# Seven products of quarter blocks in place of the last block products of a Strassen-Winograd convolution

## The chip, the cores and the metric

The kernel runs on one core of one Trainium2 chip, in 32-bit floating point. The metric is device time in microseconds for one launch, from the kernel's start to its end on that core; lower is better. Times of a kernel are the median of several runs; the profile is of one further execution.

## The reference

The input `x` has 8 images of 512 channels and 32 x 32 pixels. What is computed, cut to the steps that matter:

```
def _L0_conv_ref(x, ...):
    t = cbs(x, cv1_w, cv1_bn, 0)              # 1x1 convolution 512 -> 512, scale and shift, silu
    ys = [t[:, :C], t[:, C:]]                 # C = 256
    for i in range(2):
        yi = ys[-1]
        z = cbs(yi, m_cv1_w[i], m_cv1_bn[i], 1)           # 3x3 convolution 256 -> 256
        z = bot_attention(z, m_qkv_w[i], m_rw[i], m_rh[i]) # 4 heads of 64 over 1024 pixels
        z = silu(bn_eval(conv2d(z, m_cv2_w[i], 0), m_cv2_bn[i]))
        ys.append(yi + z)
    return cbs(concatenate(ys, axis=1), cv2_w, cv2_bn, 0)  # cv2: 1x1 convolution 1024 -> 512
x = x + _L0_conv_ref(_gn(x), ...)             # _gn: group norm
```

The change lies in the last convolution, `cv2`. Per image it is a matrix product: a weight matrix of 512 x 1024 times the four parts `ys` (1024 channels x 1024 pixels).

## The kernel before

The images are worked on in four pairs (`p` = 0 to 3, images `ia` and `ib`), one pair after another in straight code. Within a pair the order on TensorE is: 3x3 convolution 1 of both images (`conv3x3`, in a transformed domain, with loaded weights `u`), projection and attention 1 of `ia`, the same for `ib`, convolution 2, attention 2 of `ia` and of `ib`, and `cv2` of both. Where a fourth pair follows, the first 1x1 convolution `cv1` of the next pair is worked in between.

`cv2` of one image is done by Winograd's form of Strassen's method: the 512 x 1024 weights are cut into 2 x 2 blocks of 256 x 512, and the activations into 2 x 2 blocks of 512 channels x 512 pixels (`top` and `bottom`). Seven block products replace eight. Their weights are three raw blocks (`11`, `12`, `22`) and four sums (`s1` to `s4`); on the other side stand three raw blocks and the sums `t1` to `t4`. One block product (`product`, line 1338) is 8 matmuls of 128 x 128 weights by 512 columns, into one PSUM tile of two banks (`ps[:, o, :]`, one bank for each half of the outputs). Each matmul shows as two records in the profile. PSUM has three such tiles under the tag `big` and one under `av`.

For pairs 0 to 2 the function `strassen` makes the seven products in the order `11`, `s1`, `12` with `s4`, `s2`, `s3`, `22` (parts `part1`, `part2`, `part3`); it is called for `ia` first (`a1` to `a3`) and then for `ib` (`b1` to `b3`). After each of the last three, VectorE adds the whole PSUM tile to a running sum `m1` (lines 1414, 1418 and 1421, 1024 elements a partition), and lines 1416 and 1419 form two of the four output blocks from it. `finish` then applies the scale, shift and silu on ScalarE, and GpSimd's queue adds `x` with an accumulating DMA (line 1388) and stores the result (line 1389).

In the last pair (called the tail here), `rest_apart` does the same in separate steps: `m2_m3`, `m6` (`s2`), `m7` (`s3`), `m4` (`22`) for `ia`, and for `ib` `m6`, `m7` and then `m4_pieces`, which makes `22` in one piece of 512 columns and two of 256 (line 1514). The adds are lines 1493, 1498 and 1503, and 1519 for the pieces. In the tail the residual `x` of `ib` is loaded whole beforehand (`whole`, four tiles) and added on VectorE (line 1556).

Behind `b3` of pairs 0 to 2 follows the input transform of the next pair's convolution (`tiles_steps`, lines 565 to 614), on VectorE, with two small memsets on GpSimd (lines 575 and 576) for each tile of rows `w_rows`. Its third part (`i` = 2) is traced after `b3`, and its output needs the memory (`v`) that holds `y3b`, an operand of `ib`'s products `12` and `s4`.

The order on each engine is not that of the source alone. A planner goes through the program with its own estimates of durations and issues on each engine, out of what is ready by then, what comes first in the source; `tc.issue_after` adds an order by hand. The order that comes out is fixed: on the chip each engine goes through its queue in that order, and an instruction that waits holds up all behind it. The planner also puts in the waits, and gives tiles of the same tag their memory in turn. The tag `u` (`ring`) has 10 places of 4 KB a partition; weights of all kinds go through it.

Of the kernel before, what the change touches and what calls it, by code (L numbers as in the profile page):

```python
# [52 lines left out]
P = 128  # L53
# [8 lines left out]
def kernel(  # L62
# [51 lines left out]
    def ring(shape, name):  # L114
        return const.tile(shape, F32, tag="u", name=name, bufs=RING)
# [170 lines left out]
    def make_ws(a):  # L286
# [11 lines left out]

        return {f"s{i + 1}": w for i, w in enumerate(sums)}, part1, part2

    fed = {}

    def loader(key):
        kind = key[0]
        if kind == "u":
            _, n, oc, i, cp = key
            w = ring([P, NM, 2, 2, P], "u")
            nc.sync.dma_start(w, u_dram[n][oc][i][cp])
        elif kind == "sq":
            _, n, _, j = key  # L310
            at, size = SQ[j]
            w = ring([P, size, 3, P], "sq")
            nc.sync.dma_start(w, sq_dram[n][:, at : at + size])
        elif kind == "sw":
            at, size = SQ[key[2]]
            w = ring([P, size, NX // 2, C], "sw")
            nc.sync.dma_start(w, sw_dram[:, at : at + size])
        elif kind == "w1":
            w = ring([P, NX // 2, 2 * C], "w1")
            nc.sync.dma_start(w, cv1_w.rearrange("(k p) o -> p k o", p=P)[:, ts(key[2], NX // 2)])  # L320
        elif kind == "qkv":
            w = ring([P, 3 * C], "w_qkv")
            nc.sync.dma_start(w, m_qkv_w[key[1], ts(key[3], P), :])
        elif kind == "w2":
# [172 lines left out]
    def stages(act, small, ps_big, ps_av, n_pt):  # L497
# [843 lines left out]
                            skip_group_check=onto,  # L1341
                        )

        def strassen(b, ws, top, tags, tile_of):

            kept = {}

# [43 lines left out]
            def part3(bottom, after=None):  # L1391
                t1 = kept["t1"]
                t2, t3 = sums_tile("k"), tile_of("t3").rearrange("p a c (h w) -> p a c h w", w=F)
                with tc.issue_after(after.ins) if after else nullcontext():
                    for part in range(2):
                        tt(t2[:, part], bottom[1][part], t1[:, part], ALU.subtract)
                    for part in range(2):
                        tt(t3[:, part], bottom[1][part], top[1][part], ALU.subtract)
                t4 = sums_tile("q")
                for part in range(2):  # L1400
                    tt(t4[:, part], t2[:, part], bottom[0][part], ALU.subtract)
# [60 lines left out]

            return SimpleNamespace(m1=m1, t1=t1, m5=m5, kept=kept)

        def rest_apart(ws, kept, bottom, t2, t3, t4, new, finish):

            m1, m5 = kept["m1"], kept["m5"]
            pss, c12 = {}, []

            def raw(name, src, outs=range(2)):  # L1470
                if name not in pss:
                    pss[name] = ps_big.tile([P, 2, HALF], F32, tag="big", name="c_new")
                product(pss[name], ws(name), src, outs=outs)
                return pss[name]

            def m2_half():
                raw("12", bottom[0], [0])

            def m2_m3():
                raw("12", bottom[0], [1])  # L1480
                raw("s4", bottom[1])

            def add_m2():
                c11 = new()
                tt(c11, pss["12"], m1, ALU.add)
                finish(0, c11)

            def add_m3():
                c12.append(new())
                tt(c12[0], pss["s4"], m5, ALU.add)  # L1490

            def m6():
                tt(m1, raw("s2", t2), m1, ALU.add)
                tt(c12[0], c12[0], m1, ALU.add)
                finish(1, c12[0])

            def m7():
                tt(m1, raw("s3", t3), m1, ALU.add)
                tt(m5, m5, m1, ALU.add)
                finish(2, m5)  # L1500

            def m4():
                tt(m1, m1, raw("22", t4), ALU.subtract)
                finish(3, m1)

            def m4_pieces(out_of):
                flat = lambda ap: ap.rearrange("p c h w -> p c (h w)") if len(ap.shape) == 4 else ap
                t4s = [flat(t) for t in t4]
                places = [(0, 0, HALF), (1, 0, HALF // 2), (1, HALF // 2, HALF // 2)]
                for o, at, size in places:  # L1510
                    pool, tag = (ps_av, "av") if (o, at) == (1, 0) else (ps_big, "big")
                    ps = pool.tile([P, HALF], F32, tag=tag, name="c_new")[:, :size]
                    for k in range(KB):
                        nc.tensor.matmul(
                            ps, ws("22")[:, k, ts(o, P)], t4s[k // NM][:, k % NM, at : at + size],
                            start=(k == 0), stop=(k == KB - 1),
                        )
                    src = m1[:, o, at : at + size]
                    tt(src, src, ps, ALU.subtract)
                    out_of(3, o, at, size, src)  # L1520

            return SimpleNamespace(
                m2_half=m2_half, m2_m3=m2_m3, add_m2=add_m2, add_m3=add_m3, m6=m6, m7=m7, m4=m4, m4_pieces=m4_pieces
            )

        C_BLOCKS = ((0, 0), (0, 1), (1, 1), (1, 0))
# [497 lines left out]
    for p in range(NP):  # L2024
# [392 lines left out]
        if not more:  # L2417
# [14 lines left out]
            whole = [ring([P, HW], "x_res") for _ in range(NO)]  # L2432
            for oc in range(NO):
                nc.sync.dma_start(whole[oc], x[ib, ts(oc, P), :])
            ts_a = [], [], []
            rest_a = s.rest_apart(w_of, heads[ia].kept, bottom_a, *ts_a, acc_tile, s.finish_apart(ia))
# [29 lines left out]
            rest_b = s.rest_apart(w_of, heads[ib].kept, bottom, *ts_b, lambda: kept_sums.pop(0), finish)  # L2466
# [7 lines left out]
            rest_b.m2_m3()  # L2474
            rest_b.add_m2()
            rest_b.add_m3()
            rest_b.m6()
# [23 lines left out]
        b1, b1_more, b2, b3 = s.strassen(ib, w_of, top, {"m1": ("p3", 1), "m5": ("p4", 1)}, tile_of)  # L2501
        b1()
        b1_more()
        b2()
        vs = v_units()
        ecs = [{}, {}]
        for g in range(G):
# [119 lines left out]
```

## Time and profile before

| what | value |
| --- | --- |
| median of 3 runs | 2220.57 us (2220.26 to 2220.92) |
| profiled execution | 2222.78 us; its span 2221.2 us, the rest lies around it |
| TensorE (PE) busy | 2192.8 us, 99% of the span |
| VectorE (DVE) busy | 1752.2 us, 79% |
| ScalarE (ACT) busy | 1093.9 us, 49% |
| GpSimd (POOL) busy | 222.0 us, 10% |
| granted TensorE clock | 0.998 |

A busy share is that of the whole span; stages differ. PEld is TensorE's weight load, which runs beside matmuls. In a timeline a row is: start, length, engine, line, operation, output<-inputs, sizes, count, and in square brackets the idle time before it with what ended it. In a table by stage it is: from:to, length, busy time of each engine with its count of instructions, clock, the DMA engines' busy share, and GB/s.

### The profile page before, as it was taken

To read this page: it belongs to the slowest core of one execution; us is meant where nothing else is said; L and a number is where in the kernel's file an instruction comes from. 1 tells how busy PE (TensorE), PEld (TensorE's weight loads), DVE (VectorE), ACT (ScalarE), POOL (GpSimd) and SP (SyncE) were. 2 spreads that over 40 slices of the span, in tenths; PEclk is the share of its full clock that TensorE was granted. 3 is DMA by queue.
4 is the path that set the end of the run, shared out by engine and by line. 5 is a ranking of instruction groups with operands and counts; after the bars stand their busy time and mean duration, and the time that the engine had idled before them with its cause. 6 is when DMAs were issued, how large, how long until landed. Compare 5 with 4: busy or idle time off the path is not lost.

```text
span 2221.2 us, 40357 instructions
## 1 busy us (share of the span) xinstructions
PE 2192.8 (99%) x16330; PEld 1079.8 (49%) x16330; DVE 1752.2 (79%) x2794; ACT 1093.9 (49%) x1320; POOL 222.0 (10%) x416
## 2 busy tenths in 40 slices
PE   7999999999999999999999999999999999999998
PEld 3653437343474444734447443654344734383433
DVE  8988879878769688977857868987785877897664
ACT  7454553554225666465323676455622465336543
POOL 4322210000220000000021000000002100000001
PEclk9999999999999999999999999999999999999999
DMA  8954447312582324512268141542126701261123
GB/s 265 317 170 136 168 149 260 105 64 68 142 264 68 119 82 132 199 59 68 63 162 267 31 166 36 190 131 77 58 67 171 268 30 44 91 208 34 58 59 96
DMA packets 133799, 285.61 MB, mean 129 GB/s; under 512 B 33541, under 2 KB 61185, under 8 KB 132581
## 3 DMA queue, kind: packets, MB, share of 16 engines
q1 hardware_dynamic: 101700, 197.34, 26.9%
q0 software_dynamic: 31904, 85.61, 13.2%
q8 instruction: 131, 2.15, 0.4%
q14 instruction: 64, 0.52, 0.1%
HBM read 214.86 MB, written 68.03 MB: 127 GB/s over the span
## 4 chain that ended last, share of the span: by engine, by line
PE 90%; DVE 6%; issue 1%; DMA 1%; ACT 1%; POOL 0%; DVEq 0%; ACTq 0%; POOLq 0%
PE av_ps L1101 19%; PE l_ps L1064 18%; PE c_ps L659 10%; PE c L1338 9%; PE c_new L1338 8%; PE p_ps L940 7%; PE m_ps L1318 5%; PE x_ps L1579 4%; PE ps L529 4%; PE p_ps L946 3%; PE s_ps L1119 1%; DMA taps<-in_m_cv_w_dram 1%; DVE acc L1085 1%; PE p_ps L904 1%; PE pv_ps L946 0%
## 5 line engine op out<-in xcount | busy, mean ns | idle before, releaser
L1068 ACT ACTIVATE pt<-l_ps 128x1024 f32<-128x1024 f32 x512 | 495.7, 1023 | 328.1 <-PE l_ps L1064 252.2
L1064 PE MATMUL l_ps<-q,kr 64*64 64x512 f32 x4096 | 485.5, 590 | 0.9 <-ACT pt L1068 0.9
L1101 PE MATMUL av_ps<-pt,vT 64*64 64x512 f32 x4096 | 484.7, 590 | 1.3 <-DVE z L1109 1.1
L1085 DVE TENSOR_TENSOR acc<-acc,pt 128x1024 f32<-128x1024 f32 x362 | 442.8, 1223 | 37.6 <-ACT pt L1068 11.2
L1101 PEld LDWEIGHTS av_ps<-pt,vT 64*64 64x64 f32 x4096 | 156.0, 133 | 280.7 <-issue 233.9
L1064 PEld LDWEIGHTS l_ps<-q,kr 64*64 64x64 f32 x4096 | 157.5, 133 | 270.3 <-issue 246.3
L659 PEld LDWEIGHTS c_ps<-v_in,u 128*64 128x64 f32 x4320 | 235.8, 137 | 6.3 <-issue 6.0
L659 PE MATMUL c_ps<-v_in,u 128*64 128x128 f32 x4320 | 238.5, 273 | 0.0
L1109 DVE TENSOR_TENSOR z<-av_ps,z 128x512 f32<-128x512 f32 x64 | 44.0, 688 | 98.4 <-ACT z L1108 98.3
L1318 PE MATMUL m_ps<-z,m_sb 128*128 128x512 f32 x256 | 113.9, 593 | 0.0
L664 ACT COPY c_m<-c_ps 128x512 f32<-128x512 f32 x48 | 28.1, 586 | 159.6 <-PE c_ps L659 145.9
L940 PE MATMUL p_ps<-t_z,sq 128*128 128x512 f32 x224 | 105.9, 595 | 0.0
L501 ACT ACTIVATE t<-m_ps,bh,sh 128x512 f32<-128x512 f32 x64 | 46.3, 774 | 94.0 <-PE m_ps L1318 92.8
L1082 DVE TENSOR_TENSOR acc<-pt 128x1024 f32<-128x1024 f32 x64 | 78.1, 1221 | 13.8 <-PE s_ps L1119 8.3
L940 PE MATMUL p_ps<-z,sq 128*128 128x512 f32 x168 | 81.3, 604 | 0.8 <-ACT z L501 0.7
L1318 PEld LDWEIGHTS m_ps<-z,m_sb 128*128 128x128 f32 x256 | 47.7, 190 | 56.7 <-issue 51.4
L1177 DVE TENSOR_TENSOR z<-z,rs 128x512 f32<-128x512 f32 x64 | 42.5, 687 | 26.9 <-DMA rs<-r_dram 26.7
L501 ACT ACTIVATE z<-z,bh,sh 128x512 f32<-128x512 f32 x64 | 48.7, 809 | 25.4 <-DVE z L721 25.2
L940 PEld LDWEIGHTS p_ps<-t_z,sq 128*128 128x128 f32 x224 | 39.5, 191 | 36.5 <-issue 34.4
L501 ACT ACTIVATE c_out<-m_kept,bh,sh 128x512 f32<-128x512 f32 (+1 forms) x33 | 38.9, 1276 | 34.6 <-issue 16.2
L1579 PE MATMUL x_ps<-t_x,sw 128*128 128x512 f32 x128 | 55.9, 592 | 0.0
L1338 PE MATMUL c_new<-t_in,wss 128*128 128x512 f32 x128 | 55.9, 592 | 0.0
(343 smaller groups left out, 3169.6 us busy)
## 6 DMA issues: line engine op xcount, KB each, us to landing
u<-u SPq DMA_DIRECT2D x135, 512.0 KB
y_in<-y SPq DMA_DIRECT2D x32, 512.0 KB
rs<-r_dram SPq DMA_DIRECT2D x126, 128.0 KB
sq<-sq SPq DMA_DIRECT2D x42, 384.0 KB
x<-in_x_dram SPq DMA_DIRECT2D x28, 512.0 KB
r_in<-r SPq DMA_DIRECT2D x28, 512.0 KB
c_out<-in_x_dram POOLq DMA_DIRECT2D x56, 256.0 KB, 5.5
out_dram<-c_out POOLq DMA_DIRECT2D x56, 256.0 KB, 3.3
```

What stands on the lines that cost most here:

```text
L501: silued[0] = nc.scalar.activation(dst, src, AF.Silu, scale=sh[:, k : k + 1], bias=bh[:, k : k + 1])
L529: last_product[0] = nc.tensor.matmul(ps[:, half, :], w_of(k), rhs_of(k, half), start=(k == begin), stop=(k == end))
L659: conv_product[0] = nc.tensor.matmul(to[o], us[cp][:, k, row, c, o], rhs, start=(k == 0), stop=(k == NM - 1),)
L940: nc.tensor.matmul(ps[:, o, :], w[:, o, :], rhs, start=not onto, stop=True, skip_group_check=onto)
L1064: nc.tensor.matmul(ps[kh * HD : (kh + 1) * HD, hd, :], kr[r, c, o : o + HD], q[r, c, ts(half, HALF)], start=True, stop=True,)
L1068: last_exp[0] = exp = nc.scalar.activation(pt, ps, AF.Exp, scale=SCALE)
L1082: return nc.vector.tensor_tensor(accs[g], pt[0], pt[1], ALU.add)
L1085: ins = nc.vector.tensor_tensor(accs[g], accs[g], pt[i], ALU.add)
L1101: nc.tensor.matmul(avs[g][hd * HD : (hd + 1) * HD, kh, :], vT[r, j, o : o + HD], pt[i][r, hd, :], start=(j == 0), stop=(j == NJ - 1),)
L1318: nc.tensor.matmul(pss[half][:, oc, :], m2_sb[:, n, k, ts(oc, P)], ao[:, k, ts(half, HALF)], start=(k == 0), stop=(k == NM - 1),)
L1338: nc.tensor.matmul(ps[:, o, :], w[:, k, ts(o, P)], rhs[part][:, c], start=(k == 0 and not onto), stop=(k == KB - 1), skip_group_check=onto,)
L1579: nc.tensor.matmul(ps[:, o, :], w[:, c, ts(o, P)], rhs[c], start=(c == 0 and not onto), stop=(c == 1), skip_group_check=onto,)
```

## The change

The products `s2`, `s3` and `22` of `ib` in pairs 0 to 2, and in the tail `s2`, `s3`, `22` of `ia` and `s2`, `s3` of `ib`, 14 products in all, are made by `by_quarters` in place of `product`. It applies the same seven-product form once more within a block product: weights in 2 x 2 blocks of 128 x 256, activations in blocks of 256 x 256. The sums of weights (`l`, four for each of the three names) are made once in pair 0 by VectorE (`make_l`, 12 adds), stored, and loaded again by pairs 1 to 3 in place of, among others, three early loads of `u`. The sums of activations (`quarter_sums`) are four VectorE operations of 512 elements for each product. In `by_quarters` the PSUM tile's two banks hold two halves each: `z_`, `y_` in one and `x_`, `d_` in the other. VectorE adds out of PSUM in six operations: four of 256 elements (`put`) and two of 512. Two of the four `whole` tiles are loaded later, on GpSimd's queue.

```
+    def make_l(name, w):
+        t = ring([P, 4, 2, P], f"wl{name}")
+        sums_of(blocks_of(w), [t[:, i] for i in range(4)])
+        nc.gpsimd.dma_start(l_dram[name], t)
+        return t
...
+        def quarter_sums(rhs, sums):
...
+            tt(t1, b12, b11, ALU.subtract)
+            tt(t2, b22, t1, ALU.subtract)
+            tt(t3, b22, b12, ALU.subtract)
+            last = tt(t4, t2, b21, ALU.subtract)
...
+        def by_quarters(w, l, x, src, dst, op=ALU.add):
+
+            Q = HALF // 2
+            ps = ps_big.tile([P, 2, HALF], F32, tag="big", name="c_q")
+            (z_, y_), (x_, d_) = ([ps[:, bank, ts(j, Q)] for j in range(2)] for bank in range(2))
...
+            def mm(to, a, b, first=False, last=True):
+                for c in range(2):
+                    nc.tensor.matmul(
+                        to, a[:, c], b[:, c], start=first and c == 0, stop=last and c == 1, skip_group_check=True
+                    )
...
+            def put(o, j, add, how=op):
+                to, has = out(o, j)
+                return tt(to, has, add, how)
+
+            mm(x_, a11, b11, first=True)
+            put(0, 0, x_)
+            mm(y_, s1, t1, first=True)
+            put(1, 1, y_)
+            mm(d_, a22, t4)
+            put(1, 0, d_, ALU.subtract if op == ALU.add else ALU.add)
+            mm(x_, s2, t2)
+            put(0, 1, x_)
+            mm(z_, a12, b21)
+            mm(y_, s4, b22)
+            tt(dst[:, 0], dst[:, 0], ps[:, 0], op)
+            mm(x_, s3, t3)
+            low = dst[:, 1].rearrange("p (j q) -> p j q", j=2)
+            return tt(low, low, x_.unsqueeze(1).to_broadcast([P, 2, Q]), op)
...
+                quarters = {}
+                if l2:
+                    quarters = {"s2": quarter_sums(halves(t2), l2.room("s2")), "s3": quarter_sums(halves(t3), l2.room("s3"))}
...
-                tt(m1, new("s2", t2), m1, ALU.add)
+                onto("s2", t2)
+                if l2:
+                    quarters["22"] = quarter_sums(halves(t4), l2.room("22"))
...
-                tt(m1, new("s3", t3), m1, ALU.add)
+                onto("s3", t3)
...
-                tt(m1, m1, new("22", t4), ALU.subtract)
+                onto("22", t4, ALU.subtract)
...
-            ws = {name: load_ws(name) for name in ("21", "22", "11", "12")}
+            ws = {name: load_ws(name) for name in ("21", "11", "12", "22")}
...
-            feed([("ws", p, name) for name in (WS_NAMES if more else ("12", "s4", "s2", "s3", "22"))])
+            if more:
+                feed([("ws", p, name) for name in WS_NAMES])
+                feed([("wl", p, name) for name in L2_NAMES])
+            else:
+                feed([("ws", p, name) for name in ("12", "s4")])
+                feed([(kind, p, name) for name in L2_NAMES for kind in ("ws", "wl")])
...
-        if more:
-            feed(units(0)[:3])
...
             with tc.issue_after(scaled.ins):
                 rest_a.add_m3()
+                rest_a.prepare("s2")
             last = s.m2(1, z[:, :, 1], Y2[1], lambda oc, half: img(y3b[:, half, oc, :]))
...
+            rest_a.prepare("s3")
             rest_a.m6()
+            rest_a.prepare("22")
...
+            rest_b.prepare("s2")
+            rest_b.prepare("s3")
             rest_b.m2_half()
             rest_b.m2_m3()
+            for _ in range(2):
+                load_whole(nc.gpsimd)
...
         b2()
+        if p == 0:
+            for name in L2_NAMES:
+                l_made[name] = make_l(name, ws[name])
```

More of the change, by code (lines that the diff above doesn't have):

```diff
@@ L299, in make_ws, with blocks_of @@
         return {f"s{i + 1}": w for i, w in enumerate(sums)}, part1, part2
+    L2_NAMES = ("s2", "s3", "22")
+    l_dram = {name: tc.dram_tile([P, 4, 2, P], F32, name=f"l{name}") for name in L2_NAMES}
+    def blocks_of(w):
+        return [[w[:, 2 * part : 2 * part + 2, ts(o, P)] for part in range(2)] for o in range(2)]
+    def make_l(name, w):
[3 more added lines that the diff above has]
+        return t
     fed = {}
@@ L323, in loader @@
             nc.sync.dma_start(w, m_qkv_w[key[1], ts(key[3], P), :])
+        elif kind == "wl":
+            w = ring([P, 4, 2, P], f"wl{key[2]}")
+            nc.sync.dma_start(w, l_dram[key[2]])
         elif kind == "w2":
@@ L1463, in heads_apart, with rest_apart, prepare, onto @@
             return SimpleNamespace(m1=m1, t1=t1, m5=m5, kept=kept)
-        def rest_apart(ws, kept, bottom, t2, t3, t4, new, finish):
+        def rest_apart(ws, kept, bottom, t2, t3, t4, new, finish, l2):
             m1, m5 = kept["m1"], kept["m5"]
-            pss, c12 = {}, []
+            pss, c12, quarters = {}, [], {}
+            def prepare(name):
+                quarters[name] = quarter_sums({"s2": t2, "s3": t3, "22": t4}[name], l2.room(name))
+                return quarters[name].last
+            def onto(name, op=ALU.add):
+                return by_quarters(ws(name), l2.of(name), quarters[name], m1, m1, op)
             def raw(name, src, outs=range(2)):
@@ L1492, in m6 @@
             def m6():
-                tt(m1, raw("s2", t2), m1, ALU.add)
+                onto("s2")
                 tt(c12[0], c12[0], m1, ALU.add)
@@ L1497, in m7 @@
             def m7():
-                tt(m1, raw("s3", t3), m1, ALU.add)
+                onto("s3")
                 tt(m5, m5, m1, ALU.add)
@@ L2402, in w_of, with l_of, room_of @@
                 return got[name]
-        if more:
-            feed(units(0)[:3])
+        l_made = {}
+        def l_of(name):
+            if name not in l_made:
+                l_made[name] = take(("wl", p, name))
+            return l_made[name]
+        def room_of(*tiles):
+            return [t[:, j] for t in tiles for j in range(2)]
         top = load_tops(ia, None if more else Y1[0])
@@ L2430, in acc_tile, with load_whole, x_room @@
                 return act.tile([P, 2, HALF], F32, tag="acc", name="c_sum", bufs=2)
-            whole = [ring([P, HW], "x_res") for _ in range(NO)]
-            for oc in range(NO):
-                nc.sync.dma_start(whole[oc], x[ib, ts(oc, P), :])
+            whole = []
+            def load_whole(q):
+                whole.append(ring([P, HW], "x_res"))
+                q.dma_start(whole[-1], x[ib, ts(len(whole) - 1, P), :])
+            def x_room(name):
+                return room_of(*(act.tile([P, 2, 2, HALF // 2], F32, tag="x", name="t_q", bufs=NX) for _ in range(2)))
+            l2 = SimpleNamespace(of=l_of, room=x_room)
+            for _ in range(2):
+                load_whole(nc.sync)
             ts_a = [], [], []
-            rest_a = s.rest_apart(w_of, heads[ia].kept, bottom_a, *ts_a, acc_tile, s.finish_apart(ia))
+            rest_a = s.rest_apart(w_of, heads[ia].kept, bottom_a, *ts_a, acc_tile, s.finish_apart(ia), l2)
             end = s.attention_fast(qkv, z[:, :, 1], at_of(ib, 1), {NG: rest_a.m2_half})
@@ L2472 @@
                 pass
+            rest_b.prepare("s2")
+            rest_b.prepare("s3")
             rest_b.m2_half()
             rest_b.m2_m3()
+            for _ in range(2):
+                load_whole(nc.gpsimd)
             rest_b.add_m2()
@@ L2500, with room_b @@
         top = load_tops(ib)
-        b1, b1_more, b2, b3 = s.strassen(ib, w_of, top, {"m1": ("p3", 1), "m5": ("p4", 1)}, tile_of)
+        def room_b(name):
+            if name == "22":
+                t = act.tile([P, 4, 2, HALF // 2], F32, tag="k", name="t_q")
+                return [t[:, j] for j in range(4)]
+            tags = [("p1", 1), ("p2", 1)] if name == "s2" else [("x", NX)] * 2
+            return room_of(*(act.tile([P, 2, 2, HALF // 2], F32, tag=tag, name="t_q", bufs=n) for tag, n in tags))
+        b1, b1_more, b2, b3 = s.strassen(
+            ib, w_of, top, {"m1": ("p3", 1), "m5": ("p4", 1)}, tile_of, SimpleNamespace(of=l_of, room=room_b)
+        )
         b1()
```

24 lines of the change are left out of this document (20 added, 4 removed).

## The prediction, made before the changed kernel was run

> **What bounds the kernel now.** I read the page first (busy time and the chain that ended last), then who waited for whom on TensorE from 560 us on, then timelines of the places that the change touches, and a table by stage.
>
> ```profile
> PE 2192.8 (99%) x16330; PEld 1079.8 (49%) x16330; DVE 1752.2 (79%) x2794; ACT 1093.9 (49%) x1320; POOL 222.0 (10%) x416
> ...
> PE 90%; DVE 6%; issue 1%; DMA 1%; ACT 1%; POOL 0%; DVEq 0%; ACTq 0%; POOLq 0%
> ```
>
> ```profile
> PE av_ps L1101 <- DVE z L1109: 1.1, 2, 0.6
> PE l_ps L1064 <- ACT pt L1068: 0.9, 2, 0.5
> PE p_ps L940 <- ACT z L501: 0.5, 3, 0.2
> ```
>
> The first fence says that TensorE is busy 99% of the span and makes 90% of the chain. The second is its whole list of waits over 1660 us: 2.5 us. So the time is TensorE's work laid end to end, and removed TensorE time is gained if nothing else begins to hold it up. What could is seen by stage; here are `ib`'s first four products and its last three in pair 1 (rows 1 and 2), and in the tail `ia`'s last three, `ib`'s `12` with `s4`, and its `s2`, `s3`:
>
> ```profile
> 1129.29:1156.75 27.46, 27.46 (x65) 12.16 (x64) 10.10 (x11) 8.70 (x8) 7.93 (x11) 1.00 0.71 205
> 1156.75:1177.35 20.60, 20.60 (x49) 8.93 (x47) 11.46 (x18) 4.72 (x4) 3.51 (x7) 1.00 0.64 152
> 2157.73:2178.33 20.60, 20.60 (x50) 9.12 (x49) 9.66 (x9) 6.17 (x6) 3.83 (x5) 1.00 0.24 47
> 2178.33:2192.06 13.73, 13.73 (x34) 6.08 (x32) 6.10 (x6) 4.79 (x4) 4.98 (x7) 1.00 0.78 180
> 2192.06:2205.79 13.73, 13.73 (x33) 6.08 (x32) 5.06 (x5) 2.38 (x2) 0.00 (x0) 1.00 0.11 43
> ```
>
> Columns: stage, length, PE, PEld, DVE, ACT, POOL. TensorE fills every stage at full clock; VectorE has 7 to 17 us free in each. That free time is what the change spends.
>
> **The change part by part.** *TensorE.* The start of a block product to the start of the next, and the matmuls of 256 columns that the tail has already:
>
> ```profile
> 1156.75 7.03 PE L1338 MATMUL c_new<-t_in,wss 128*128 128x512 f32 x16
> 1163.62 7.03 PE L1338 MATMUL c_new<-cz,wss 128*128 128x512 f32 x16
> ```
>
> ```profile
> 2205.79 7.05 PE L1514 MATMUL c_new<-t_in,ws 128*128 128x512 f32 x24
> ```
>
> ```profile
> L1514 PE MATMUL c_new<-t_in,ws x24: 379/379/592, 2205.8 to 2212.5; 128*128 128x256 f32 x16, 128*128 128x512 f32 x8
> ```
>
> A product takes 1163.62 - 1156.75 = 6.87 us, 0.43 us for each of 16 records. The pieces of line 1514 take 7.05 us from the first start to the last end: 8 records of 512 columns (3.43 us), 16 of 256, the last of which shows 0.38. That leaves 7.05 - 3.43 - 0.38 = 3.24 us for 15 spacings, 0.216 us a record, with full 128 x 128 weights loaded each time. The new form is 7 x 2 matmuls, 28 records: 28 x 0.216 = 6.05 us. It saves 0.82 us a product, 14 x 0.82 = 11.5 us in all if TensorE never waits.
>
> *VectorE.* Durations and spacing by size, the last three rows with PSUM as a source in 1519:
>
> ```profile
> 1084.04 0.41 DVE L607 SCALAR_TENSOR_TENSOR v_in<-w_d 128x256 f32<-128x256 f32 x1
> 1084.36 0.42 DVE L608 SCALAR_TENSOR_TENSOR v_in<-w_d 128x256 f32<-128x256 f32 x1
> ...
> 2210.46 0.68 DVE L1519 TENSOR_TENSOR m_kept<-m_kept,c_new 128x512 f32<-128x512 f32 x1
> 2211.05 0.69 DVE L1556 TENSOR_TENSOR c_out<-c_out,x_res 128x512 f32<-128x512 f32 x1
> 2211.66 0.42 DVE L1519 TENSOR_TENSOR m_kept<-m_kept,c_new 128x256 f32<-128x256 f32 x1
> ```
>
> ```profile
> 1143.22 1.22 DVE L1401 TENSOR_TENSOR t_in<-t_in,ypad 128x1024 f32<-128x1024 f32 x1 [6.16 <-PE c L1338]
> 1144.36 1.22 DVE L1401 TENSOR_TENSOR t_in<-t_in,y3b 128x1024 f32<-128x1024 f32 x1
> ```
>
> Back to back that is 0.33 us for 256 elements, 0.60 for 512, 1.14 for 1024. Each product adds four of 512 (`quarter_sums`, 2.4 us) and puts four of 256 and two of 512 (2.5 us) in place of one of 1024: +1.4 us there. Sum 3.8 us a product, 53 us in all, none of it on the path by itself. The 12 adds of `make_l` (256 elements, 4 us) fall once into pair 0, where `ib`'s first products leave as much VectorE time free as in row 1; its three stores are GpSimd issues of under 1 us with nothing urgent behind them. If that cover were gone, they would cost 4 us once. That `22` is loaded last of four in pair 0 moves one 512 KB load behind others of its kind, long before the sums are made: no cost.
>
> *The ping-pong.* Before, TensorE needed VectorE only to free a tile, of which there are three. Now `d_` and the second `x_` follow adds out of the same bank. How long such a turn takes:
>
> ```profile
> 1136.15 7.03 PE L1338 MATMUL c<-t_in,wss 128*128 128x512 f32 x16
> 1143.02 3.60 PE L1338 MATMUL c<-ypad,ws 128*128 128x512 f32 x8
> ```
>
> ```profile
> 1352.46 0.68 DVE L1109 TENSOR_TENSOR z<-av_ps,z 128x512 f32<-128x512 f32 x1
> ```
>
> ```profile
> 1353.20 1.52 PE L1101 MATMUL av_ps<-pt,vT 64*64 64x512 f32 x12 [0.55 <-DVE z L1109]
> ```
>
> TensorE could go on at 1143.02, and line 1401 (above) began at 1143.22: 0.20 us. From the end of 1109 (1353.14) to the matmul is 0.06. With an add of 0.42 a turn is 0.68 us. One step of the new product is 4 records, 0.86 us. So one step in between covers a turn, with 0.18 us to spare and only if VectorE is free at that moment; an operation of 0.6 or 1.2 us just begun uses the spare up. In source order the second `x_` stands right behind `d_`, in the same bank, with no step between. Whether the planner keeps that order is seen in how it filled a gap before:
>
> ```profile
> 1087.97 1.88 PE L1318 MATMUL m_ps<-z,m_sb 128*128 128x512 f32 x4
> 1089.69 1.02 PE L1338 MATMUL c<-ypad,ws 128*128 128x512 f32 x2
> 1090.56 5.42 PE L1318 MATMUL m_ps<-z,m_sb 128*128 128x512 f32 x12
> ```
>
> One matmul of `12` stands inside `m2`, ahead of its place in the source. I therefore expect it to put `z_` ahead of the second `x_`, which restores one step between any two uses of a bank, and to put the next product's first steps into what is left open.
>
> No row of before shows two engines at one bank, so whether the waits are by bank must be bounded: nothing if they are not, 0.68 us a product if they are and the order is kept. [...]
>
> *Pairs 0 to 2.* The sums for `s2` and `s3` (4.8 us) fit into the 17.4 us free in row 1. Those for `22` use the memory of `t2` (tag `k`), so they fall into row 2's stage. VectorE then has 11.46 + 3 x 1.4 + 2.4 = 18.1 us in a stage for which TensorE wants 3 x 6.05 = 18.1. And it does not run through: `w_d` of the next convolution waits for a memset that stands in GpSimd's queue behind a store, which waits for a DMA.
>
> ```profile
> 1160.63 0.58 POOL L1389 DMA_DIRECT2D out_dram<-c_out  x1 [3.60 <-DMA c_out<-in_x_dram]
> 1161.20 0.18 POOL L575 MEMSET w_rows<- 128x32 f32 x1
> 1163.14 0.56 POOL L1389 DMA_DIRECT2D out_dram<-c_out  x1 [1.76 <-DMA c_out<-in_x_dram]
> 1163.69 0.18 POOL L576 MEMSET w_rows<- 128x32 f32 x1
> ```
>
> ```profile
> 1161.41 0.69 DVE L603 TENSOR_TENSOR w_d<-w_rows 128x512 f32<-128x512 f32 x1 [1.89 <-POOL w_rows L575]
> 1163.90 0.69 DVE L604 TENSOR_TENSOR w_d<-w_rows 128x512 f32<-128x512 f32 x1 [1.80 <-POOL w_rows L576]
> ```
>
> Before, this idle 3.7 us cost nothing, as TensorE had a whole spare tile. Now adds stand in VectorE's queue behind these two, and TensorE waits for the adds. Upper bound of the stage: 18.1 + 3.7 = 21.8 us of VectorE against 20.6 before, a loss of 1.2. Lower bound: 18.1, a gain of 2.5. The third part of the input transform comes later in the source than the adds; the operations behind `w_d` there (some 2.6 us) can slide into the convolution. So I take 19.9, nearer the middle: a gain of 0.7, three times, 2.1 us.
>
> *The tail.* Ideal gain 5 x 0.82 = 4.1 us. VectorE's new work is 5 x 3.8 = 19 us against 10.9 + 7.6 + 8.7 = 27.2 free, and no memset is in its way. `ia`'s three products are the tight place (9.66 + 4.2 + 2.4 for `22`, and up to 4.8 of `s3` and of `ib`'s sums, against 18.1). Their adds will be late by part of a 0.6 to 1.2 us operation. I take 0.3 us of waiting a product, between 0 and the 0.68 of a whole turn: 1.5 us, so the tail gains 2.6. The two late `whole` tiles are needed only by the last two output blocks, over 10 us after they can be issued: no cost; if late, up to a few us at the end.
>
> *Loads.* Three loads of `u` lose their early place in each of three transitions.
>
> ```profile
> 1143.21 48.79 SPq L308 DMA_DIRECT2D u<-u  x14
> ```
>
> ```profile
> 1177.35:1209.00 31.65, 31.65 (x577) 31.42 (x576) 26.80 (x50) 8.82 (x12) 8.58 (x13) 1.00 0.99 338
> ```
>
> The convolution (second row) lasts to 1209.00 and the last `u` is issued at 1192.0. Three of 512 KB, 1.5 MB at the 338 GB/s of that row, are 4.7 us, against some 10 us until the last third of the convolution wants them. Places in `ring` come free with `11`, `s1`, `12` and `s4` before the convolution starts, enough for its first four; the loads of `wl` take the bytes that the three of `u` had at the earlier place. On the SP queue the three are moved behind the loads of the next pair's activations and of `ib`'s `top`, which are wanted sooner anyway. No cost.
>
> **Sum.** 2.1 + 2.6 = 4.7 us. The profiled execution's own time is 2222.78 (span 2221.2 and 1.6 around), so 2218.1 for it; it stands 2.2 us above the median, and for the median I forecast 2220.57 - 4.7 = 2215.9.
>
> **The rivals.** *Nearly all of it* (chance 0.23): the planner's order leaves room and the waits for memsets fall where no add stands behind them. For: VectorE's free time in the rows by stage. Against: a spare of 0.18 us. 2220.57 - 11.5 = 2209.1, up to 2213.
>
> *It is given back* (0.21): the order is kept as written, or VectorE bounds both stages: 2.0 us of gain or less, 2218.6; with the stage of pairs 0 to 2 at 21.8 (+3.6) and the tail at 0.68 a product (-0.7), 2223.5. Against: the row of line 1338 inside `m2`.
>
> *Slower: the convolution starves* (0.12): the DMA engines are 0.99 busy there. If the three displaced loads (4.7 us) and the next pair's `x`, whose memory (tag `x`) now holds quarter sums, come behind everything else, and the 10 us of cover is in truth under 4.7, TensorE waits up to 4.7 us in each of three transitions: 2215.9 + 14.1 = 2230; it decides from a wait of 3 us each, 2225. Against: no wait for a DMA in the list of waits.
>
> **How the numbers follow.** My own case (0.44, part of the gain, 2213 to 2218.6) is the likeliest: 2215.9. A measurement of this kernel can tell 0.2%, 4.4 us, from no change: 2216.1 and 2225.0 are the borders. Faster: 0.23 and somewhat over half of 0.44, 0.50. Slower: nearly all of 0.12 and a little of the given back, 0.13. The rest, 0.37, is within. The range from 2209.5 to 2223.5 runs from near the bound of the first rival to that of the second, and leaves out the last rival and some hundredths at the lower end, under 0.2 together.
>
> **What would show it.** 28 records a product at 0.215 us. In TensorE's waits new entries on adds into `m1`, about 0.3 us a product in the tail and 1.8 us a stage in pairs 0 to 2, most of them just after a `w_d` that waited for a memset. `z_` ahead of the second `x_`. `u` issued later, with no wait of `c_ps` on a DMA. I am wrong if VectorE's order puts line 603 and 604 behind the adds (then faster), or if `c_ps` waits (then slower).

## The result and the profile after

The changed kernel takes 2292.68 us (median of 4 runs, 2289.35 to 2294.9) against 2220.74 us before (4 runs on the same chip): 1.0322 times as long, 95% interval 1.0304 to 1.0340. It is slower by 72 us, and the forecast of 2215.9 us was wrong. The lines of the code up to `product` are 15 further down than before (its matmul is 1353), later ones more; 1384 is the matmul of `by_quarters`, 1393 its `put`, 1405 and 1408 its two adds of 512.

Busy time and the chain that ended last:

```profile
PE 2211.7 (97%) x16498; PEld 1115.6 (49%) x16498; DVE 1810.7 (79%) x2932; ACT 1094.5 (48%) x1320; POOL 224.8 (10%) x421
...
PE 73%; DVE 12%; DMA 6%; issue 5%; ACT 1%; POOL 1%; SPq 0%; DVEq 0%; POOLq 0%; ACTq 0%
```

TensorE, whose list of waits behind 560 us held 2.5 us before, now waits for VectorE (line, who for whom: us in total, times, longest):

```profile
PE c_q L1384 <- DVE m_kept L1393: 23.9, 22, 4.2
PE c_q L1384 <- DVE m_kept L1405: 9.4, 12, 0.8
PE c_ps L674 <- DVE m_kept L1408: 4.7, 6, 0.8
PE g_ps L2652 <- DVE m_kept L1602: 3.1, 1, 3.1
```

The table by stage, from `ib`'s `cv2` to the next projection in pairs 0 to 2, and the tail to the end of the span; before, and after:

```profile
534.80:666.10 131.30, 131.30 (x810) 75.36 (x809) 95.02 (x154) 32.86 (x35) 26.35 (x47) 1.00 0.62 183
2140.50:2221.20 80.70, 72.46 (x182) 33.40 (x178) 38.79 (x48) 22.93 (x22) 11.73 (x16) 0.97 0.34 86
```

```profile
534.90:683.80 148.90, 139.19 (x848) 85.37 (x844) 107.20 (x182) 33.16 (x35) 26.33 (x47) 0.95 0.60 176
1095.40:1242.00 146.60, 136.22 (x845) 82.85 (x845) 107.23 (x182) 33.16 (x35) 26.31 (x47) 0.98 0.60 180
1653.50:1803.60 150.10, 139.81 (x848) 85.82 (x845) 107.31 (x182) 33.12 (x35) 26.34 (x47) 0.94 0.60 173
2192.20:2289.00 96.80, 72.59 (x238) 43.20 (x238) 58.97 (x93) 22.76 (x22) 12.73 (x18) 0.95 0.32 83
618.80:622.30 3.50, 0.01 (x1) 0.00 (x0) 1.07 (x3) 0.00 (x0) 0.73 (x2) 1.00 0.51 195
623.35:637.00 13.65, 11.58 (x60) 9.00 (x60) 7.22 (x14) 2.37 (x2) 1.76 (x2) 0.50 0.29 81
```

```profile
1183.14:1189.97 6.83, 5.86 (x12) 3.70 (x12) 3.49 (x9) 0.00 (x0) 0.00 (x0) 0.50 0.17 38
1739.51:1756.58 17.07, 13.30 (x63) 9.91 (x63) 9.40 (x18) 2.37 (x2) 2.35 (x4) 0.50 0.26 80
```

Pairs 0 to 2 took 131.3 us each (1 and 2 within 0.1 of 0); now they take 17.6, 15.3 and 18.8 more. The tail takes 16.1 more. That is 67.8 us, the growth of the span (2221.2 to 2289.0); the sums of the weights (below) and a shorter start, some 2 us each, cancel before the first of these stages. The clock, 1.00 in every stage of pairs before, is under 1 in all three. The place in pair 0, TensorE and VectorE:

```profile
617.68 1.13 PE L1384 MATMUL c_q<-t_q,ws_s 128*128 128x256 f32 x4
622.31 1.13 PE L1384 MATMUL c_q<-t_q,wls 128*128 128x256 f32 x4 [3.49 <-DVE m_kept L1393]
623.95 2.07 PE L1384 MATMUL c_q<-t_in,ws_s 128*128 128x256 f32 x4 [0.51 <-DVE m_kept L1393]
...
628.51 2.07 PE L1384 MATMUL c_q<-t_q,wls 128*128 128x256 f32 x4 [0.78 <-DVE m_kept L1405]
631.36 5.38 PE L674 MATMUL c_ps<-v_in,u 128*64 128x128 f32 x46 [0.78 <-DVE m_kept L1408]
```

```profile
621.23 0.69 DVE L619 TENSOR_TENSOR w_d<-w_rows 128x512 f32<-128x512 f32 x1 [2.45 <-POOL w_rows L591]
621.84 0.41 DVE L1393 TENSOR_TENSOR m_kept<-m_kept,c_q 128x256 f32<-128x256 f32 x1
...
623.48 0.42 DVE L1393 TENSOR_TENSOR m_kept<-m_kept,c_q 128x256 f32<-128x256 f32 x1
```

Three things are to be seen. First, the step at 623.95 is `z_`, which writes the bank of `z_` and `y_`. It begins 0.05 us after the add at 623.48, and that add reads `x_`, in the other bank. Likewise the last step (628.51, into `x_`) waits for the add of both upper quarters, which reads the other bank. Second, the add of `d_` (621.84) stands in VectorE's queue behind a `w_d` that waits for a memset of GpSimd: TensorE idles 3.49 us. Third, 1.0 us after TensorE goes on, its clock is 0.50, for 13.65 us; in pairs 1 and 2 for 6.83 and 17.07 us.

### The profile page after: what moved, and what is told of

The parts are those of the page before. It is cut to its first block, busy times and chain, and to the rows that moved or that the text cites. A ratio compares the mean times of both kernels' runs of the same rounds, so it can differ in the third digit from the quotient of the medians.

```text
span 2289.0 us, 40869 instructions
## 1 busy us (share of the span) xinstructions
PE 2211.7 (97%) x16498; PEld 1115.6 (49%) x16498; DVE 1810.7 (79%) x2932; ACT 1094.5 (48%) x1320; POOL 224.8 (10%) x421
## 4 chain that ended last, share of the span: by engine, by line
PE 73%; DVE 12%; DMA 6%; issue 5%; ACT 1%; POOL 1%; SPq 0%; DVEq 0%; POOLq 0%; ACTq 0%
PE av_ps L1116 18%; PE l_ps L1079 17%; PE c_ps L674 10%; PE p_ps L955 6%; PE x_ps L1662 4%; PE c_q L1384 4%; PE m_ps L1333 4%; DMA c_out<-in_x_dram 3%; PE ps L544 3%; PE p_ps L961 3%; PE c L1353 2%; DVE acc L1100 1%; PE s_ps L1134 1%; PE c_new L1353 1%; DMA rs<-r_dram 1%
## 5 line engine op out<-in xcount | busy, mean ns | idle before, releaser
L674 PE MATMUL c_ps<-v_in,u 128*64 128x128 f32 x4320 | 248.1, 276 | 5.0 <-DVE m_kept L1408 4.7
L674 PEld LDWEIGHTS c_ps<-v_in,u 128*64 128x64 f32 x4320 | 241.5, 139 | 16.1 <-issue 8.1
L516 ACT ACTIVATE c_out<-cz,bh,sh 128x512 f32<-128x512 f32 x12 | 14.4, 1302 | 102.4 <-DVE cz L1492 102.4
L1393 DVE TENSOR_TENSOR m_kept<-m_kept,c_q 128x256 f32<-128x256 f32 x56 | 23.4, 418 | 45.4 <-PE c_q L1384 45.3
L1384 PE MATMUL c_q<-t_q,wls 128*128 128x256 f32 x120 | 37.0, 435 | 22.0 <-DVE m_kept L1393 15.0
```

The lines of the kernel that those rows point to most:

```text
L516: silued[0] = nc.scalar.activation(dst, src, AF.Silu, scale=sh[:, k : k + 1], bias=bh[:, k : k + 1])
L674: conv_product[0] = nc.tensor.matmul(to[o], us[cp][:, k, row, c, o], rhs, start=(k == 0), stop=(k == NM - 1),)
L1384: nc.tensor.matmul(to, a[:, c], b[:, c], start=first and c == 0, stop=last and c == 1, skip_group_check=True)
```

## The experiments

Theory 1: every step of a product waits for the add before it, since all four quarters lie in one PSUM tile and the wait is by tile. Theory 2: VectorE's queue, blocked by the memset, makes the loss. The half clock (0.50 for 13.65 us in pair 0) follows the idle time of either.

**e1, no adds in between.** `put(0, 0, x_)`, `put(1, 1, y_)`, `put(1, 0, d_, ...)` and `put(0, 1, x_)` are taken out.

> Leaves out the four adds of a quarter product that stand between its steps (the puts at 00, 11, 10 and 01); the two last adds of 512 columns stay, so the output lacks those four terms. Theory 1 (each step of a product waits for the add before it, because all four quarters lie in one PSUM tile and the wait goes by the tile): the 0.5 to 0.94 us in front of the steps go, one wait a product is left (the last step behind the add of both upper quarters, about 0.8 us), 14 x 0.8 = 11 us; 2292.7 less some 60 to 70 us, 2220 to 2235. Theory 2 (VectorE's queue, blocked by the difference that waits for GpSimd's memset, makes nearly all of the loss, with the clock that halves behind it): the blocked add is then one of the two that stay, the three stalls of about 3.5 us stay, and 2270 to 2290 is expected. Theory 3 (quarter matmuls themselves are slower in these stages, or PSUM tiles are short): 28 records take more than 6.05 us without any add, and the time stays above 2260.

Measured 2234.63 us (1.0061, 1.0044 to 1.0077): 58 us gone, at the upper end of the range of theory 1 and far from theory 2 alone. Of TensorE's waits on adds five are left: one of 3.7 to 4.0 us in each pair, behind the blocked queue, and two of 0.6 to 0.7 us in the tail:

```profile
PE c_q L1384 <- DVE m_kept L1401: 13.0, 5, 4.0
```

**e2, two PSUM tiles a product.**

```
-ps = ps_big.tile([P, 2, HALF], F32, tag="big", name="c_q")
-(z_, y_), (x_, d_) = ([ps[:, bank, ts(j, Q)] for j in range(2)] for bank in range(2))
+ps, ps_x = (ps_big.tile([P, 2, HALF], F32, tag="big", name=name) for name in ("c_qz", "c_qx"))
+(z_, y_), (x_, d_) = ([t[:, 0, ts(j, Q)] for j in range(2)] for t in (ps, ps_x))
```

> The quarters z and y in one PSUM tile, x and d in another, order of the source kept. Theory 1 (waits by the whole tile): only the second x still follows an add directly, about 0.8 us a product (14 x 0.8 = 11 us), and the three stalls of 3.5 us with their half clock stay (10 us and 13 us): 2209 + 11 + 23, about 2243, range 2232 to 2255. The prediction's own reading (waits by the bank): the two tiles change nothing, since z and y had a bank of their own before, and the time stays at 2285 to 2295. Theory 2 (blocked VectorE queue): within 5 us of 2292.7. Theory 5 (PSUM tiles are short): two tiles a product instead of one make it worse, above 2295.

Measured 2243.69 us (1.0108, 1.0091 to 1.0125): 49.0 us gone by an edit that leaves `z_` with `y_` in one bank and `x_` with `d_` in another, as they were. Theory 1 stands, and by theory 5, too few PSUM tiles, it would have become slower. The waits, and the order in pair 0:

```profile
PE c_qx L1384 <- DVE m_kept L1393: 18.6, 10, 3.1
```

```profile
617.38 1.03 PE L1384 MATMUL c_qz<-t_in,ws_s 128*128 128x256 f32 x4
618.25 1.06 PE L1384 MATMUL c_qx<-t_q,wls 128*128 128x256 f32 x4
```

With two tiles the planner does put `z_` (617.38) ahead of the second `x_` (618.25), as the prediction had expected.

**e3, two tiles and z first in the source.** `mm(z_, a12, b21)` moves in front of `mm(x_, s2, t2)`.

> As the kernel with two PSUM tiles, and z's step moved in front of the second x in the source, so that any two uses of a tile have a step between them. Theory 1: the serial turn of 0.8 us a product goes too, 11 us less than the kernel with two tiles: about 2232, range 2220 to 2243, with the three stalls behind the memset and their half clock left in it. Theory 2: within 5 us of 2292.7. By the prediction's reading (bank waits, with the order that it had assumed): 2212 to 2219.

Measured 2243.25 us (1.0100, 1.0083 to 1.0116): no gain over e2, and theory 1's 11 us were wrong. The rows above say why: the planner had made that move already.

**e4, the memset on VectorE.** `nc.gpsimd.memset` becomes `nc.vector.memset` for the third part of the transform, the rest is the change.

> The kernel after the change, with the two memsets of the row buffer ahead of the third part of the input transform made by VectorE instead of GpSimd, so that the difference of the transform no longer waits behind GpSimd's store. Theory 2: nearly all comes back, 2215 to 2235. Theory 1: only the three stalls of 3.5 to 4.2 us with the half clock behind them, 10 us and up to 13 us: 2269 to 2283, and the waits of 0.5 to 0.9 us in front of the steps stay as they are.

Measured 2271.35 us (1.0230, 1.0212 to 1.0247): 21.3 us gone, as theory 1 said, and the waits on 1405 stay word for word as they were (9.4, 12, 0.8). Pair 0 now runs at a clock of 1.00 (0.95 with the change) and takes 140.4 us in place of 148.9, and 131.3 before:

```profile
534.20:674.60 140.40, 133.68 (x849) 81.43 (x845) 107.31 (x187) 33.16 (x35) 25.71 (x43) 1.00 0.64 188
```

**e5, two tiles and the memset.**

> Two PSUM tiles a product, order of the source, and the memsets ahead of the third part of the transform on VectorE. The kernel with two tiles alone took 2243.7 us; in each of pairs 0 to 2 it waits some 4.6 us behind the blocked difference and loses some 1.7 us more at half clock. Theory 1 with theory 2 (the waits by tile and the memset are two separate costs that add up): 3 x 6.3 = 19 us come back, 2225, range 2219 to 2230; what is left lies in the tail (about 4 us over before) and in the sums of the weights (about 2 us). Rival (VectorE as such is too full in the stages, the memset only showed where): at most 8 us come back, 2236 or more, and TensorE's waits on the adds stay above 10 us in all.

Measured 2234.78 us (1.0056, 1.0040 to 1.0073): 8.9 us under e2, not 19, and between the ranges of theory and rival. The two stand on different chips, where the kernel before took 2222.18 and 2220.53 us; against it the difference is 10.6 us. Another wait is left close by: in each pair TensorE idles 2.47 us in front of `d_` of `s3` (1.4 to 2.2 us in e2). e6 shows what it waits for.

**e6, first image of the tail plain, weight sums on GpSimd.** `sums_of(..., nc.gpsimd.tensor_tensor)` in `make_l`, and `rest_apart` of `ia` with `product` in place of `by_quarters`.

> As the kernel with two tiles and the memsets on VectorE; the twelve sums of the weights' quarters are made by GpSimd instead of VectorE, and the tail's first image makes its three products plainly, as before the change, so that the tail has two quarter products, those of the second image. Theory (VectorE is the bound only around the first image's three products in the tail, and the weights' sums cost about 2.3 us once because they stand in front of the softmax sums): 2225 less 2.3 and less 5 to 6 (the tail's TensorE part then is 72.4 less 2 x 0.82): 2217, range 2213 to 2221. Rival (quarter products in pairs 0 to 2 do not gain even without stalls): 2221 to 2226.

Measured 2232.15 us (1.0043, 1.0026 to 1.0060): a miss. The tail gained the 6 us expected (71.9 us to the start of its last matmul, 77.9 in e5). The miss is in the pairs, which take 134.0 to 134.3 us, against 131.3 before. VectorE, then TensorE, in pair 0:

```profile
614.11 0.69 DVE L621 SCALAR_TENSOR_TENSOR v_in<-w_d 128x512 f32<-128x512 f32 x1 [11.37 <-PE c L1353]
...
620.01 0.69 DVE L1366 TENSOR_TENSOR t_q<-t_in 128x512 f32<-128x512 f32 x1
...
623.02 1.22 DVE L1492 TENSOR_TENSOR cz<-c,m_kept 128x1024 f32<-128x1024 f32 x1
624.15 0.68 DVE L621 SCALAR_TENSOR_TENSOR v_in<-w_d 128x512 f32<-128x512 f32 x1
624.75 0.41 DVE L1393 TENSOR_TENSOR m_kept<-m_kept,c_qx 128x256 f32<-128x256 f32 x1
```

```profile
625.22 1.94 PE L1384 MATMUL c_qx<-t_q,ws_s 128*128 128x256 f32 x4 [2.47 <-DVE m_kept L1393]
```

The first add of `s3` (624.75) stands behind the four sums for `22` (from 620.01) and the output block `c12` (623.02, line 1492). The sums come so late because they use `t2`'s memory, which `s2` reads until then; e9 tests this.

**e7, the tail's sums on GpSimd.** `quarter_sums(..., nc.gpsimd.tensor_tensor)` in the tail, all five products by quarters.

> As the kernel with two tiles and the memsets on VectorE; the twelve sums of the weights' quarters and, in the tail, the four sums of each quarter product are made by GpSimd (1.28 us for one of 512 columns in this kernel, 0.60 on VectorE). Theory (VectorE, busy without a gap from 2170 to 2206 us in the tail, is the bound there): five products' sums, 12 us, leave it, the tail's TensorE part falls from 76.1 to 69 to 72 and the weights' 2.3 us go: 2225 - 2.3 - 5 = 2217, range 2213 to 2221. Rival (GpSimd's chain of three sums, 3.8 us a product, and its stores become what TensorE waits for): a new wait on lines 1366 to 1369 by GpSimd, 2224 or more.

Measured 2234.23 us (1.0051, 1.0034 to 1.0068): 0.6 us under e5, with the weight sums moved as well. Most of the miss lies in the pairs, which take 133.9 to 134.3 us as in e6. The tail takes 75.4 us to the start of its last matmul, against 77.9 in e5 and 72.3 before, and TensorE still waits 1.2 to 1.6 us at single steps, each time for VectorE; no wait names GpSimd's sums, as the rival had it. Beside GpSimd's sums an add of 1024 elements on VectorE took up to 2.30 us in place of 1.22 (last section). So the bound in the tail stays open, and this move doesn't make it gain.

**e8, one tile, z first**: the change with e3's move alone.

> The kernel after the change with one edit: z's step stands in front of the second x, in the same single PSUM tile. This is the order that the prediction had assumed. Theory 1 (waits by the tile): nothing changes, 2285 to 2297, since each step still waits for the add before it whichever bank that add reads. The prediction's reading (waits by the bank, the order was what failed): 2213 to 2235.

Measured 2292.11 us (1.0315, 1.0265 to 1.0365), from two runs of 2282.67 and 2301.55: no gain that can be told, and both far from the 2213 to 2235 of waits by bank. `z_` does stand ahead of the second `x_` (652.67 and 653.64 in pair 0's `22`) and waits 0.51 us for the add of `d_`, in the other bank. The order that the prediction had counted on gives nothing while the wait is by tile.

**e9, sums of `22` early.** On e6:

```
-t = act.tile([P, 4, 2, HALF // 2], F32, tag="k", name="t_q")
-return [t[:, j] for j in range(4)]
+t = act.tile([P, 2, 2, HALF // 2], F32, tag="x", name="t_q", bufs=NX)
+return room_of(tile_of("t_q"), t)          # a free quarter of cz, and t
```

and `quarters["22"] = ...` moves from behind `onto("s2", t2)` to behind the sums of `t4`.

> As the kernel with the plain first image in the tail, and the quarter sums for `22` lie in memory of their own (a free quarter of cz and a tile x) instead of t2's, so that VectorE can make them 20 us earlier, while it idles. That kernel (2232.2 us) has one stall left in each of pairs 0 to 2: 2.47 us before the d of `s3`, whose add stands in VectorE's queue behind these four sums (2.4 us), behind c12 (1.2) and a step of the transform (0.6), with 3.4 us of half clock behind it (1.7 us lost). Theory (what is left is the order of VectorE's queue): 2.4 of the 2.47 us go, and with them the half clock: 3 x 4.1 = 12 us, 2220, range 2217 to 2225. Rival (the chain from the last step of `s2` over c12 to the first add of `s3` carries the stall, with or without the sums): 0.9 us of 2.47 stay, no half clock, 2223 to 2226. Rival (the memory of x makes the loads of the next pair late): 2230 or more.

Measured 2220.92 us (0.9998, 0.9988 to 1.0007): 11.2 us gone (10.1 against the kernel before on each chip), 12 expected; the granted clock of its runs is 0.997 to 0.999, as in the kernel before on that chip, and 0.996 or 0.997 in e6.

**e10, `s3` into a tile of its own.** The adds of `s3` write into a tile `u2` in place of the running sum, so they need not wait for `c12`, which reads that sum: `onto("s3", t3, to=u2)` with `u2` under tag `p1`, then `onto("22", t4, ALU.subtract, has=u2)`.

> As the kernel with early sums for `22`, and the product of `s3` writes its four quarters into a tile of its own (p1) instead of m1, from which `22` then goes back into m1. So its first add no longer waits for c12 (1.2 us), which reads m1. Theory: no wait of TensorE on an add over 0.5 us in pairs 0 to 2, their stage from the first product to the next projection falls from 134.0 to 129 to 130 us (131.3 before the change), 2232.2 - 3 x 4.5 = 2218.7, range 2215 to 2222, that is at or just under the kernel before. Rival (c12 stands in the queue all the same, as it is older): no difference to the kernel with early sums alone.

Measured 2217.51 us (11 runs; 0.9987, 0.9978 to 0.9996). Of all waits on adds of quarter products one is left, in the tail:

```profile
PE c_qx L1384 <- DVE m_kept L1393: 0.8, 1, 0.8
```

**e11, e10 with one PSUM tile again.**

> As the kernel with s3 in a tile of its own, but with the four quarters of a product in one PSUM tile again, as in the change. It prices the wait by tile alone, with every other stall gone. Theory 1: the steps of a product are serial with the adds again. One tile against two took 140.3 against 132.3 us a pair where the memset alone was mended, 8 us, three times, and the tail's two products lose 1 to 3 us each: 2217.5 + 24 + 4 = 2245, range 2236 to 2255. Rival (once VectorE's queue is in order, the wait by tile costs little, since the planner puts other steps between): under 2228.

Measured 2249.80 us (1.0129, 1.0111 to 1.0148), 32.3 us more than e10. The two differ in the lines of the PSUM tile alone. Pair 0 and the tail, in e10 and then in e11:

```profile
533.20:662.90 129.70, 129.69 (x849) 82.01 (x845) 106.77 (x190) 32.96 (x35) 25.87 (x43) 1.00 0.64 191
2133.90:2215.70 81.80, 71.01 (x202) 37.79 (x202) 46.92 (x66) 22.78 (x22) 12.30 (x17) 0.95 0.36 92
```

```profile
535.10:671.40 136.30, 132.96 (x849) 81.47 (x845) 107.34 (x186) 33.14 (x35) 25.73 (x43) 1.00 0.62 188
2156.20:2250.40 94.20, 75.44 (x202) 39.02 (x202) 47.03 (x66) 22.43 (x22) 12.28 (x17) 0.88 0.31 80
```

The pairs, at full clock, take 136.3, 136.8 and 136.1 us against 129.7, 129.6 and 129.5 in e10: 20.4 us for nine products, 2.3 us each, is the wait by tile alone. The tail takes 94.2 against 81.8 for two products, at a mean clock of 0.88 against 0.95.

**e12, pairs 0 to 2 only.** e10 with the tail as before the change.

> As the kernel with s3 in a tile of its own, with the tail as before the change: no quarter products there, and all four tiles of the last residual loaded early. The tail's two products gain 0.6 us of TensorE there (71.8 against 72.4) and its end after the last matmul is 1.7 us longer (10.0 against 8.3). Expected 2217.5 + 0.6 - 1.7 = 2216.4, range 2214.5 to 2219. If the longer end does not come from the tail's products, 2218.

Measured 2216.37 us (11 runs; 0.9980, 0.9971 to 0.9989). It is the lowest median of all, 4.3 us (0.2%) under the kernel before. e10, on another chip, is 1.1 us above it; their intervals overlap, so the two can't be told apart. Its pairs:

```profile
533.00:662.60 129.60, 129.59 (x844) 81.93 (x844) 106.76 (x190) 32.97 (x35) 25.89 (x43) 1.00 0.64 191
1074.40:1203.90 129.50, 129.50 (x844) 81.95 (x844) 106.65 (x190) 33.14 (x35) 25.93 (x43) 1.00 0.64 191
1615.50:1745.00 129.50, 129.50 (x844) 82.04 (x844) 106.66 (x185) 33.02 (x35) 25.91 (x43) 1.00 0.64 191
```

TensorE fills each, and each is 1.7 to 1.9 us shorter than before.

## Why the prediction was wrong

**The step that failed: "waits are by bank".** The prediction bounded the ping-pong by nothing and by one turn of 0.68 us a product. Both ends took for granted that steps in the two banks go on side by side. The trace has the turn about as forecast: 0.51 us idle in front of a step behind an add of 256, 0.78 behind one of 512, and 1.64 us from one step to the next (2216.55 to 2218.19 in the rows of the tail below) in place of 0.86, so 0.78 a turn. But there are up to five turns in a product, since in the rows above a step waits for the last add out of its tile, whichever quarters that reads (0.51 us at 623.95, 0.78 at 628.51). e2 (49.0 us) and e11 (2.3 us a product even where the planner fills in) show it. The assumed order did not come either: in the changed kernel `z_` (623.95) stands behind the second `x_` (622.31). e8 shows that with one tile it would not have helped. So the single turn of 0.68 us a product, from which the 2.0 us of gain in "given back" come, was no upper bound here: no run shows a wait by bank, and the runs show waits by tile. Nor does a run show what the chip would do with finer waits, since the waits are set when the kernel is built; two tiles were the way to get them.

**The blocked queue: right place, too small.** The prediction named the `w_d` behind GpSimd's memset and took 1.8 us a stage. It was 3.49 us at one stroke in pair 0 and up to 4.2 elsewhere. What it left out is the clock: it was forecast as full throughout. 13.65, 6.83 and 17.07 us at 0.50, with 11.58 us of matmuls in the first, lost half of the latter, an estimated 5.8 us (a step of four records shows 2.07 us there, at 623.95, and 1.13 just before, at 622.31). So the stall and the half clock behind it cost some 9.3 us in pair 0, 2.7 times the stall; e4, without them, takes 8.5 us less there. And "what is late next" was not asked: with the memset gone, the sums for `22` and `c12` stood at the same place (e5, e6), which the prediction's sum of VectorE's work for the stage could not show, since VectorE was idle 11.4 us right before and then late by 2.5.

**The sums of the weights: the cover was not there.** They were costed at nothing with 4 us as the price without cover. TensorE waited 2.1 us in pair 0's attention, where no wait stood before; with the sums on GpSimd (e6) the first of these waits is gone and the second is 0.2 us:

```profile
PE s_ps L1134 <- DVE acc L1100: 1.5, 1, 1.5
PE av_ps L1116 <- DVE z L1124: 0.6, 1, 0.6
```

**The tail: 0.3 us of waiting a product** was forecast, and a gain of 2.6; it lost 16.1 us. Where other matmuls stand between the steps (`ib`'s `12` and `s4` beside `ia`'s `s3` and `22`) there is next to no wait; where none is left, at `ia`'s `s2` and at the very end, nearly every step waits:

```profile
2214.48 1.13 PE L1384 MATMUL c_q<-t_q,wls 128*128 128x256 f32 x4 [2.24 <-DVE m_kept L1393]
2216.55 1.13 PE L1384 MATMUL c_q<-t_q,wss 128*128 128x256 f32 x4 [0.94 <-DVE m_kept L1393]
2218.19 1.13 PE L1384 MATMUL c_q<-t_q,wls 128*128 128x256 f32 x4 [0.51 <-DVE m_kept L1393]
...
2278.68 0.19 PE L2652 MATMUL g_ps<-ones,good 128*1 128x1 f32 x2 [3.09 <-DVE m_kept L1602]
```

**What held.** VectorE's work grew by 58.5 us (1752.2 to 1810.7), against 53 and 4 forecast. The matmuls are 28 records at 0.215 us (a step of four each 0.86 us, 638.82 to 639.68 in e2), and with every wait out of the way the gain is there: 1.8 us a pair, 0.6 a product, against 0.82 forecast; where the rest went was not traced. The loads of `u` cost nothing: behind 560 us `c_ps` waits 4.7 us in all for adds (line 1408) and never for a DMA, so the rival that ended slower did so by a mechanism that did not occur. Nearest was "given back", which had the order as written and the wait, but one turn of it.

## What to carry to other kernels

When a product is cut into smaller steps that hand results to another engine through PSUM, look at which tile each wait names, and give steps that are to overlap tiles of their own; here sharing a bank or not did not show in the waits, sharing a tile did (49.0 us went in e2 with the banks as they were). Then read the consumer's queue, not its free time: a sum of busy time per stage says nothing about which instruction stands in front of the add that TensorE waits for, so move what can be done early (memory of its own), and cut chains through one accumulator (a second one). And price a stall of TensorE at more than its length where the clock may halve behind it, as it did behind 2.47 us in e6 and 3.49 us in the changed kernel.

## What the runs showed of the hardware

**The clock halved behind 2.47 us of idle time.** The clock's changes lie on a grid of 3.41 us: the stretches at half clock above, 13.65, 6.83 and 17.07 us, are 4, 2 and 5 times that. In e6 a window, one step of that grid, with 0.94 us of matmuls is followed by one at half clock; in e5 a window with 1.54 us is not (tables of the windows, cut on that grid, of e6 and of e5, each with the next one):

```profile
621.98:625.39 3.41, 0.94 (x5) 0.52 (x4) 3.41 (x6) 1.12 (x2) 0.11 (x1) 1.00 0.59 215
625.39:628.81 3.42, 3.42 (x9) 2.71 (x10) 2.63 (x8) 1.24 (x2) 1.76 (x2) 0.50 0.39 63
```

```profile
624.09:627.50 3.41, 1.54 (x8) 1.00 (x6) 3.41 (x6) 0.35 (x1) 0.19 (x1) 1.00 0.79 245
627.50:630.91 3.41, 2.81 (x13) 2.50 (x14) 3.31 (x10) 2.04 (x2) 1.76 (x2) 1.00 0.24 28
```

A gap shorter than a window was enough in e6: 2.47 us, all within the first window (622.75 to 625.22). In e5 the gap has the same 2.47 us, of which 1.87 are idle time of the first window above and 0.60 of the next, and the clock stayed at 1.00. Coming back took more than staying did in e5 (1.54 us): in pair 2 of the changed kernel four windows with 1.72 to 2.91 us of matmuls at half clock were each followed by another, and only the fifth, with 3.42 us, by full clock (1739.51 to 1756.58); in pair 1 the second, with 2.96 us, was (1183.14 to 1189.97).

**Adds of VectorE and of GpSimd took longer side by side.** In e7, with GpSimd's sums beside it, an add of 1024 with both sources in SBUF took 2.30 us in place of 1.22 (at 2168.20, with GpSimd idle), and GpSimd's add of 512 up to 2.26 in place of 1.28:

```profile
2154.91 2.30 DVE L1510 TENSOR_TENSOR t_in<-t_in,y_half 128x1024 f32<-128x1024 f32 x1
...
2171.58 0.41 DVE L1393 TENSOR_TENSOR m_kept<-m_kept,c_qx 128x256 f32<-128x256 f32 x1
```

```profile
2171.27 1.51 POOL L1366 TENSOR_TENSOR t_q<-t_in 128x512 f32<-128x512 f32 x1 [6.27 <-PE c_qx L1384]
L1369 POOL TENSOR_TENSOR t_q<-t_q,t_in x3: 1278/2252/2263, 2153.9 to 2176.2; 128x512 f32<-128x512 f32 x3
```

The add out of PSUM (2171.58, beside the GpSimd sum of 2171.27, which ends at 2172.78) kept its 0.41.
